# Eight single PSUM banks in place of one group of four and four singles, and experts by blocks of 512 tokens queued beside a line of attentions

## The chip, the core and the metric

The kernel runs on one core of a Trainium2 chip. The core has five engines with queues of their own: PE (TensorE, with its weight loads shown apart as PEld), DVE (VectorE), ACT (ScalarE), POOL (GpSimd) and SP (SyncE, which only issues DMAs here). The metric is device time in microseconds of one execution, lower is better. All arithmetic is in float32, but for a mask that is added in bfloat16.

## The reference

The input is x with 8 sequences of 256 tokens and 128 features, so 2048 rows. Two layers are computed, each an attention and then a mixture of experts. Cut to what matters:

```
# layer 0
q, (k, v) = rope(LN(x) Wqa Wqb), LN(x) Wkva Wkvb       # 16 heads of 8, 4 heads of keys and values
x = x + softmax(q k^T / sqrt(8), causal, per sequence of 256) v Wout + bout
p = softmax(LN(x) gate_W); the two largest of 8 experts, weights scaled to sum 1
o = 0.5 gelu(LN(x) shared_W + shared_b) + sum over the two of weight * (gelu(LN(x) W1[e] + b1[e]) W2[e] + b2[e])
x = x + LN(o) * gamma + beta
# layer 1
xl = LN(x); linear attention over segments of 32 tokens (q, k through elu + 1), normalised, Wo
gates = softmax over the means of earlier segments and a running mean; x += what the gates retrieve
p = softmax(LN(x) gate_w + gate_b); the two largest of 8 experts
x = x + sum over the two of (relu(LN(x) w1[e] + b1[e]) w2[e] + b2[e])
```

The hidden width of an expert is 512. The output has the shape of x.

## The kernel before

Rows are held in four blocks of 512 tokens (`xs[0..3]`, NT = 4 tiles of 128 rows each). A block is two sequences, and layer 0's attention goes sequence by sequence ("row" in the code, eight of them), with heads on the four 32-row groups of the PE.

Attention of layer 0 (`Row`, `attention0`): `maxima` computes the scores of a row once (`scores`, L586, and L592 adds the causal mask), and DVE takes the row maxima from PSUM in one instruction over 2048 columns (L608). `weighted` computes the transposed scores again with the maxima folded in, ACT takes Exp of 2048 columns in one instruction (L637), PE multiplies by the values (L640), DVE copies out (L648), PE picks the columns apart (L651), DVE normalises (L659), PE transposes (L663) and projects (L509). Each row yields three times in `weighted`, and at each of these the maxima of the next row go a step on.

Attention of layer 1 (`attention1`, one block at a time): a projection into four banks (L748), scores per tile into four banks (L877), a mask on DVE over 2048 columns (L881), values (L891, L905), and the retrieval (L938, L946, L952).

Experts: `route0` and `route1` choose two experts for each token. `dispatch` gives each chosen (token, expert) pair a slot of its own in a DRAM buffer (`xg`), where tiles of 128 slots belong to one expert, and POOL scatters the rows there by indirect DMA, 128 rows each (L368). `experts` goes over the tiles: SP reads the number of the tile's expert into a register and loads both weights of that expert, 512 KB in all (L424, L425); PE computes the hidden layer (L431) and the output (L446); ACT (Gelu, and Relu for even chunks) or DVE (Relu for odd chunks) reads the hidden layer out (L441, L439); each four tiles are copied out by DVE (L454) and stored to `yg`. `chosen` gathers them by indirect DMA (L480), and `combine0` or `combine1` adds them to the rows.

Before, the unit of routing is a half of 1024 tokens (HB = 2 blocks). Its number of tiles is fixed: 2048 pairs in 16 tiles plus up to 7 tiles that are begun for an expert and not filled, SL = 23. Two halves in two layers make 92 tiles.

PSUM has eight banks of 512 float32 columns. Before, four of them are one group that scores and layer 1's projection take as a whole, and four are single:

```
ps4 = ctx.enter_context(tc.tile_pool(name="ps4", bufs=1, space=PSUM))
ps1 = ctx.enter_context(tc.tile_pool(name="ps1", bufs=4, space=PSUM))
```

The order of work is set by generators that are woven by hand and by the framework's scheduler, which fixes one order for each engine's queue. `weave(one, other, rate, lead=n)` takes `rate` steps of `other` for each step of `one`, after n steps; a step of `experts` is one tile.

```
weave(first, none, 0.0, stop=HB - 1)
weave(first, chain(moe0(0), second(0)), 1.5, lead=3)
weave(second(1), moe0(1), 2.0, lead=2)
weave(chain(second(2), second(3)), moe1(0), 1.0, lead=2)
weave(moe1(1), finished(0), 0.2, lead=6)
```

So the attention of blocks 0 and 1 runs with no experts beside it, blocks 2 and 3 have experts of the first half beside them, `second(b)` is layer 1 of block b up to its routing, and the experts of the last half stand at the end, with only the last additions behind them.

Of the kernel before, what the change touches and what calls it, by code (L numbers as in the profile page):

```python
# [22 lines left out]

# [16 lines left out]
P = 128  # L40
# [14 lines left out]
HB = 2  # L55
HT = HB * NT
SL = 2 * HT + E - 1
# [9 lines left out]
    "before": P, "ones": P, "cap": E * HT, "upto": E * E, "slot": SL, "index": E,  # L67
# [10 lines left out]
def two_layers(  # L78
# [13 lines left out]
    ps4 = ctx.enter_context(tc.tile_pool(name="ps4", bufs=1, space=PSUM))  # L92
    ps1 = ctx.enter_context(tc.tile_pool(name="ps1", bufs=4, space=PSUM))
# [10 lines left out]
    def quad():  # L104

        return tl(ps4, [P, G, 512], "sc")
# [90 lines left out]
    for h in range(NBLK // HB):  # L197
# [66 lines left out]
    def small(tag, shape=(P, NT, E)):  # L264
        return tl(sm, list(shape), tag)
# [43 lines left out]
    class Half:  # L309


        def __init__(self, h):
            self.h = h
            self.rows = tl(wk, [P, HT, D], "hrows")
            self.hots = tl(wk, [P, 2, HT, E], "hhots")
            self.gates = tl(wk, [P, 2, HT], "hgates")

    def dispatch(half, b1s):

        h1, h2 = half.hots[:, 0], half.hots[:, 1]  # L320
        m, tot = small("chosen", (P, HT, E)), small("total", (P, E))
# [3 lines left out]
        rank = pr[:, 0 : HT * E].rearrange("p (t e) -> p t e", e=E)  # L325
        nc.tensor.matmul(rank, lhsT=const("before"), rhs=m, start=True, stop=False)
        for t in range(HT - 1):
            n = HT - 1 - t
            nc.tensor.matmul(
                rank[:, t + 1 :, :], lhsT=const("ones"),  # L330
                rhs=m[:, t, :].unsqueeze(1).to_broadcast([P, n, E]),
                start=False, stop=(t == HT - 2),
            )
# [3 lines left out]
        c3, tiles = small("cap3", (P, E, HT)), small("tiles", (P, E))  # L337
        nc.vector.tensor_tensor(
            c3, last(pc[:, 0:E], HT), const("cap").rearrange("p (e c) -> p e c", e=E), ALU.is_gt
        )  # L340
        nc.vector.tensor_reduce(tiles, c3, AX.X, ALU.add)
        u3, ends, starts = small("upto3", (P, E, E)), small("ends", (P, E)), small("starts", (P, E))
# [7 lines left out]
        base, pos = small("base", (P, E)), small("pos", (P, HT, E))  # L350
        nc.vector.tensor_scalar_mul(base, starts, float(P))
        nc.vector.tensor_tensor(
            pos, rank, base.unsqueeze(1).to_broadcast([P, HT, E]), ALU.add
        )
        ph, at = small("posk", (P, 2, HT, E)), small("at", (P, 2, HT))
        nc.vector.tensor_tensor(
            ph, half.hots, pos.unsqueeze(1).to_broadcast([P, 2, HT, E]), ALU.mult
        )
        nc.vector.tensor_reduce(at, ph, AX.X, ALU.add)
        half.slots = tl(wk, [P, 2, HT], "slots", mybir.dt.uint32)  # L360
# [5 lines left out]
        for t in range(HT):  # L366
# [22 lines left out]
        half.expert = tl(wk, [P, SL], "expert", mybir.dt.int32)  # L389
        nc.vector.tensor_copy(half.expert, of)  # L390
        half.bias = tl(wk, [P, SL, NC], "bias")
# [83 lines left out]
    def chosen(half, i):  # L475

        yt = tl(wk, [P, 2, NT, D], "yt", bufs=1)
        for t in range(NT):
            for k in range(2):
                nc.gpsimd.indirect_dma_start(  # L480
                    out=yt[:, k, t, :], out_offset=None, in_=yg[half.h][:, :],
                    in_offset=bass.IndirectOffsetOnAxis(
                        ap=half.slots[:, k, i * NT + t : i * NT + t + 1], axis=0
                    ),
                )
# [17 lines left out]
    def project(oT_bank, w):  # L503

        oT = tl(wk, [P, 2 * P], "oT")
        nc.scalar.copy(oT, oT_bank[:, 0 : 2 * P])
# [17 lines left out]
    class Row:  # L524
# [55 lines left out]
        def scores(self, lhsT, rhs, mask):  # L580

            sc = quad()
            for j in range(KVH):
                rows = slice(32 * j, 32 * j + 32)
                with follow(j):
                    nc.tensor.matmul(  # L586
                        sc[:, j, :], lhsT=lhsT[rows], rhs=rhs[rows], start=True, stop=mask is None
                    )
            for j in range(KVH):
                if mask is not None:  # L590
                    with follow(1):
                        nc.tensor.matmul(  # L592
                            sc[:, j, :].rearrange("p (i k) -> p i k", i=G), lhsT=identb, rhs=mask,
# [4 lines left out]
        def maxima(self):  # L598

            for qt in range(2):  # L600
                nms = []
                for kt in range(qt + 1):
                    nm = small(f"nmax{kt}", (P, KVH, G))
# [4 lines left out]
                    nc.vector.tensor_reduce(  # L608
                        nm, sc.rearrange("p j (i k) -> p j i k", i=G), AX.X, ALU.max, negate=True
                    )  # L610
                    nms.append(nm)
                    if kt == qt:
                        dst = self.qx[:, qt, :, :, HD].rearrange("p i j -> p j i")
                        if qt:
                            nc.vector.tensor_tensor(dst, *nms, ALU.min)
                        else:
                            nc.vector.tensor_copy(dst, nms[0])
                    yield

        def weighted(self):  # L620
            oT_bank = bank()
            for qt in range(2):
# [9 lines left out]
                for kt in range(qt + 1):  # L632
# [4 lines left out]
                    nc.scalar.activation(pT, sc, AF.Exp)  # L637
# [12 lines left out]
                for i in range(G):  # L650
# [12 lines left out]
                nc.tensor.transpose(  # L663
                    oT_bank[:, qt * P : (qt + 1) * P], on.rearrange("p j i d -> p (j i d)"), ident
                )
                if qt:
                    pw = project(oT_bank, wout_s)
# [22 lines left out]
    def route0(x, half, i):  # L690
        xn = half.rows[:, i * NT : (i + 1) * NT, :]
# [3 lines left out]
        hots = half.hots[:, :, i * NT : (i + 1) * NT, :]  # L695
# [5 lines left out]
        for k, m in enumerate((m1, m2)):  # L701
            g = half.gates[:, k, i * NT : (i + 1) * NT]
# [17 lines left out]
    def combine0(x, half, i, acc):  # L720
        yt = chosen(half, i)
        for t in range(NT):
            for k in range(2):
                nc.vector.scalar_tensor_tensor(
                    acc[:, t, :], yt[:, k, t, :], half.gates[:, k, i * NT + t : i * NT + t + 1],
# [8 lines left out]
    def attention1(x):  # L734
# [12 lines left out]
        for t in range(NT):  # L747
            nc.tensor.matmul(  # L748
                pp[:, t, :], lhsT=xlT[:, t * P : (t + 1) * P], rhs=wqkvu, start=True, stop=True
            )  # L750
        for t in range(NT):
            nc.scalar.activation(
                s2[:, t].rearrange("p a d -> p (a d)"), pp[:, t, 0 : 2 * D],
# [366 lines left out]
```

## Time and profile before

| what | value |
|---|---|
| time, median of 3 runs | 1099.59 us (1095.2 to 1102.19) |
| the profiled execution, own time | 1101.3 us |
| its span, first to last instruction | 1099.5 us |
| PE busy | 655.6 us (60%), weight loads 444.6 us (40%) |
| DVE busy | 423.0 us (38%) |
| ACT busy | 243.8 us (22%) |
| POOL busy | 211.5 us (19%) |
| mean granted PE clock | 0.697 of full speed |
| DMA | 76.35 MB, mean 69 GB/s |

The page lists, for each line of the kernel, how often an instruction ran, its busy time and mean duration, and the idle time just before it with what ended it. A 40-slice strip shows when each engine was busy and which clock the PE was granted. Windows give the same numbers for stretches that the reader chooses, in microseconds from the span's start; waits list who waited for whom. A busy share over the whole span mixes stages with different limits, so the stages are read one by one.

### The profile page before, as it was taken

How to read it: one execution, taken by the hardware profiler on the slowest of the kernel's cores; microseconds unless marked ns; L12 is line 12 of the kernel's file. 1: busy time of each engine (PE TensorE's matmuls, PEld its weight loads, DVE VectorE, ACT ScalarE, POOL GpSimd, SP SyncE). 2: the span in 40 equal slices, each digit the busy share in tenths (PEclk: the TensorE clock that was granted, in tenths of full speed). 3: DMA queues.
4: the chain of work that ended last, by engine and by line, in shares of the span. 5: the costliest groups of instructions: out<-in, count | busy, mean ns of one | idle time of the engine just before them, and what ended most of it. 6: DMA issues, size and time to landing. Idle time of an engine off the chain costs nothing.

```text
span 1099.5 us, 11701 instructions
## 1 busy us (share of the span) xinstructions
PE 655.6 (60%) x4154; PEld 444.6 (40%) x4170; DVE 423.0 (38%) x1121; ACT 243.8 (22%) x505; POOL 211.5 (19%) x267
## 2 busy tenths in 40 slices
PE   3666555655566677775138649873059759730970
PEld 2222221324122454465115427773037647630970
DVE  4422433235131513041246545442247657541431
ACT  1212121201213434431121014341022122200320
POOL 5000100003300000006440220104721120166005
PEclk9856557655565868876665559995559869955995
DMA  7000000001200222314400004743204413214861
GB/s 213 1 0 1 0 1 1 1 1 52 82 0 20 77 58 58 89 53 129 133 14 1 1 0 129 206 117 112 62 6 135 125 46 87 66 48 134 261 207 55
DMA packets 103786, 76.35 MB, mean 69 GB/s; under 512 B 7520, under 2 KB 89776, under 8 KB 103728
## 3 DMA queue, kind: packets, MB, share of 16 engines
q1 hardware_dynamic: 98304, 66.04, 20.8%
q0 software_dynamic: 4096, 8.40, 2.4%
q10 hardware_dynamic: 1328, 1.17, 0.4%
q8 instruction: 33, 0.54, 0.2%
q14 instruction: 25, 0.20, 0.1%
HBM read 61.30 MB, written 14.29 MB: 69 GB/s over the span
## 4 chain that ended last, share of the span: by engine, by line
PE 48%; DVE 18%; POOL 10%; ACT 9%; issue 8%; DMA 5%; another core or an unknown queue 1%; SPq 0%; POOLq 0%; ACTq 0%; DVEq 0%
PE sc L586 7%; PE mm L431 7%; PE mm L446 6%; DVE nmax L608 5%; POOL yt L480 4%; ACT at L637 4%; PE sc L592 3%; PE mm L640 3%; POOL xg L368 3%; PE sc L748 2%; PE sc L877 2%; PE mm L891 2%; DMA w<-in_w 2%; PE mm L497 2%; PE mm L905 1%
## 5 line engine op out<-in xcount | busy, mean ns | idle before, releaser
L441 ACT ACTIVATE hT<-mm,bias 128x128 f32<-128x128 f32 x276 | 84.9, 371 | 234.9 <-PE mm L431 198.1
L446 PE MATMUL mm<-w,hT 128*128 128x128 f32 x736 | 114.1, 295 | 18.4 <-issue 11.8
L431 PE MATMUL mm<-xrT,w 128*128 128x128 f32 x736 | 117.1, 314 | 6.9 <-DVE xrT L415 6.0
L431 PEld LDWEIGHTS mm<-xrT,w 128*128 128x128 f32 x736 | 106.3, 224 | 17.9 <-DVE xrT L415 10.4
L446 PEld LDWEIGHTS mm<-w,hT 128*128 128x128 f32 x736 | 100.8, 206 | 26.0 <-issue 13.7
L608 DVE TENSOR_REDUCE nmax<-sc 128x16 f32<-128x2048 f32 x24 | 55.0, 2291 | 109.4 <-PE sc L586 71.7
L480 POOL DMA_INDIRECT yt<-yg,slots x64 | 62.3, 974 | 102.9 <-DMA yg<-ys 58.9
L368 POOL DMA_INDIRECT xg<-hrows,slots x64 | 66.6, 1040 | 79.1 <-DVE slots L361 60.8
L640 PE MATMUL mm<-at,vx 128*32 128x512 f32 x192 | 37.7, 871 | 48.9 <-ACT at L637 48.9
L637 ACT ACTIVATE at<-sc 128x2048 f32<-128x2048 f32 x24 | 45.1, 1877 | 81.7 <-PE sc L592 69.7
L586 PE MATMUL sc<-qm,kxT 32*128 32x512 f32 x192 | 42.6, 970 | 25.5 <-DVE nmax L608 16.6
L223 POOL TENSOR_SCALAR rsqrt<-mv 128x4 f32<-128x4 f32 (+1 forms) x24 | 6.1, 254 | 256.2 <-DVE mv L233 251.1
L648 DVE COPY os<-mm 128x512 f32<-128x512 f32 x16 | 11.1, 691 | 113.4 <-PE mm L640 102.0
L251 PE MATMUL mm<-ident,xl 128*128 128x128 f32 x16 | 4.1, 404 | 80.9 <-DVE xl L240 80.9
L955 POOL TENSOR_TENSOR x<-x,hr 128x128 f32<-128x128 f32 x16 | 7.4, 465 | 229.8 <-DVE x L928 216.2
L439 DVE TENSOR_SCALAR hT<-mm,bias 128x128 f32<-128x128 f32 x92 | 31.4, 348 | 36.5 <-ACT hT L441 36.2
L586 PE MATMUL sc<-km,qT 32*128 32x512 f32 x192 | 43.0, 982 | 1.7 <-DVE nmax L608 1.7
L881 DVE TENSOR_TENSOR at<-sc,consts 128x2048 f32<-128x2048 f32 x16 | 36.6, 2287 | 13.7 <-PE sc L877 13.6
L415 DVE COPY xrT<-mm 128x512 f32<-128x512 f32 (+1 forms) x24 | 15.9, 664 | 55.1 <-PE mm L413 34.1
L492 PE MATMUL mm<-ident,gates 128*8 128x128 f32 x32 | 8.1, 407 | 48.5 <-DVE gates L967 21.3
L413 PE MATMUL mm<-ident,xr 128*128 128x128 f32 x92 | 17.8, 325 | 30.8 <-DMA xr<-xg 30.8
L251 PEld LDWEIGHTS mm<-ident,xl 128*128 128x128 f32 x16 | 2.6, 180 | 82.0 <-issue 47.5
(214 smaller groups left out, 1081.3 us busy)
## 6 DMA issues: line engine op xcount, KB each, us to landing
w<-in_w SPq DMA_DIRECT2D x184, 256.0 KB
xr<-xg SPq DMA_DIRECT2D x20, 256.0 KB
yg<-ys SPq DMA_DIRECT2D x20, 256.0 KB
xg<-zero SPq DMA_DIRECT2D x10, 256.0 KB
x<-in_x SPq DMA_DIRECT2D x4, 256.0 KB
xg<-hrows,slots POOLq DMA_INDIRECT x64
yt<-yg,slots POOLq DMA_INDIRECT x64
out<-x SPq DMA_DIRECT2D x4, 256.0 KB
```

Of the source, the lines that this page charges most:

```text
L368: i = nc.gpsimd.indirect_dma_start(out=xg_h[:, :], out_offset=bass.IndirectOffsetOnAxis(ap=half.slots[:, k, t : t + 1], axis=0), in_=half. ...
L431: nc.tensor.matmul(ph[:, c * P : (c + 1) * P], lhsT=w1s[:, c * P : (c + 1) * P], rhs=xrT[:, t * P : (t + 1) * P], start=True, stop=True,)
L439: nc.vector.tensor_scalar(hT[:, c, :], src, bias, 0.0, ALU.add, ALU.max)
L441: nc.scalar.activation(hT[:, c, :], src, func, bias=bias)
L446: nc.tensor.matmul(po[:, t * D : (t + 1) * D], lhsT=hT[:, c, :], rhs=w2s[:, c, :], start=(c == 0), stop=(c == NC - 1),)
L480: nc.gpsimd.indirect_dma_start(out=yt[:, k, t, :], out_offset=None, in_=yg[half.h][:, :], in_offset=bass.IndirectOffsetOnAxis(ap=half.slot ...
L586: nc.tensor.matmul(sc[:, j, :], lhsT=lhsT[rows], rhs=rhs[rows], start=True, stop=mask is None)
L592: nc.tensor.matmul(sc[:, j, :].rearrange("p (i k) -> p i k", i=G), lhsT=identb, rhs=mask, start=False, stop=True,)
L608: nc.vector.tensor_reduce(nm, sc.rearrange("p j (i k) -> p j i k", i=G), AX.X, ALU.max, negate=True)
L637: nc.scalar.activation(pT, sc, AF.Exp)
L640: nc.tensor.matmul(po[32 * j : 32 * j + 32, :], lhsT=self.vx[:, kt, j, :], rhs=pT[:, j, :], start=(kt == 0), stop=(kt == qt),)
L881: nc.vector.tensor_tensor(at.rearrange("p j i k -> p (j i) k"), sc.rearrange("p j (i k) -> p (j i) k", i=G), const("tri").unsqueeze(1).to_ ...
```

## The change

It has two parts.

First, PSUM: the group of four goes, `ps1` has eight buffers, and `quad()` returns four single banks. All that read 2048 columns at once now reads 512 at a time: row maxima (four reductions in place of one), Exp (four in place of one), the mask of layer 1 (four in place of one), the product of the retrieval (four in place of two); the copy of `u` in layer 1 goes from one DVE instruction to four on ACT. The transposes of the normalised heads, which held a bank through a whole row, move into `project`, at the end of the row.

Second, the experts: the unit of routing is a block of 512 tokens, SL = 2 * 4 + 7 = 15 tiles, and four blocks in two layers make 120 tiles. Each block scatters 8 times and gathers 8 times. The experts of a block go into a queue (`Line`), and each step of an attention lets the queue go on by 2.7 tiles (layer 0) or 1.2 tiles (layer 1). A block's experts may start 4 units after it was dispatched; its gather is issued 2 units after its last tile.

```diff
-HB = 2
-HT = HB * NT
-SL = 2 * HT + E - 1
+SL = 2 * NT + E - 1
...
-    ps4 = ctx.enter_context(tc.tile_pool(name="ps4", bufs=1, space=PSUM))
-    ps1 = ctx.enter_context(tc.tile_pool(name="ps1", bufs=4, space=PSUM))
+    ps1 = ctx.enter_context(tc.tile_pool(name="ps1", bufs=8, space=PSUM))
...
     def quad():
-        return tl(ps4, [P, G, 512], "sc")
+        return [bank() for _ in range(G)]
...
-    def project(oT_bank, w):
+    def project(heads, w):
+        pt = bank()
+        for t in range(2):
+            nc.tensor.transpose(pt[:, t * P : (t + 1) * P], heads[t], ident)
...
-                    nc.vector.tensor_reduce(
-                        nm, sc.rearrange("p j (i k) -> p j i k", i=G), AX.X, ALU.max, negate=True
-                    )
+                    for j in range(KVH):
+                        nc.vector.tensor_reduce(
+                            nms[kt][:, j, :], sc[j].rearrange("p (i k) -> p i k", i=G), AX.X,
+                            ALU.max, negate=True,
+                        )
...
-                    nc.scalar.activation(pT, sc, AF.Exp)
+                    for j in range(KVH):
+                        nc.scalar.activation(pT[:, j, :], sc[j], AF.Exp)
...
-        nc.vector.tensor_copy(u, pp[:, :, 3 * D :])
+            nc.scalar.copy(u[:, t, :], pp[t][:, 3 * D :])
...
-                nc.vector.tensor_tensor(
-                    at.rearrange("p j i k -> p (j i) k"),
-                    sc.rearrange("p j (i k) -> p (j i) k", i=G),
-                    const("tri").unsqueeze(1).to_broadcast([P, H, P]), ALU.mult,
-                )
+                for j in range(G):
+                    nc.vector.tensor_tensor(
+                        at[:, j], sc[j].rearrange("p (i k) -> p i k", i=G),
+                        const("tri").unsqueeze(1).to_broadcast([P, G, P]), ALU.mult,
+                    )
...
+    class Line:
+        def __init__(self):
+            self.now, self.credit, self.queue, self.later = 0.0, 0.0, deque(), deque()
+
+        def add(self, steps, then):
+            self.queue.append((self.now + LAG, steps, then))
+
+        def go(self, n):
+            self.now += n
+            while self.later and self.later[0][0] <= self.now:
+                self.later.popleft()[1]()
+            self.credit += n
+            while self.queue and self.queue[0][0] <= self.now and self.credit >= 1.0:
+                _, steps, then = self.queue[0]
+                if next(steps, self) is self:
+                    self.queue.popleft()
+                    self.later.append((self.now + LAG / 2, then))
+                else:
+                    self.credit -= 1.0
+            if not (self.queue and self.queue[0][0] <= self.now):
+                self.credit = 0.0
...
+    def beside(steps, n, stop=None):
+        for mark in steps:
+            line.go(n)
+            if stop is not None and mark == stop:
+                return
+
     first = layer0()
-    weave(first, none, 0.0, stop=HB - 1)
-    weave(first, chain(moe0(0), second(0)), 1.5, lead=3)
-    weave(second(1), moe0(1), 2.0, lead=2)
-    weave(chain(second(2), second(3)), moe1(0), 1.0, lead=2)
-    weave(moe1(1), finished(0), 0.2, lead=6)
-    for _ in finished(1):
-        pass
+    for b in range(NBLK - 1):
+        beside(first, 2.7, b)
+    beside(layer1(0), 1.2)
+    beside(first, 2.7)
+    for b in range(1, NBLK):
+        beside(layer1(b), 1.2)
+    while line.queue or line.later:
+        line.go(1)
```

`layer0` and `layer1` route and dispatch each block and put its experts on the line; the gather of layer 0 is issued when a block's experts are done (`fetch`), and at the end of layer 1 a block is gathered, added and stored (`finish`). The buffers that must live from dispatch to gather (`slots`, `hgates`, `expert`, `bias`) have four copies.

## The prediction

> **What bounds the kernel now.** I read the page's first and second part, then cut the span into its stages with windows, then asked the waits of the stages one by one. First the strip and the windows (columns: stretch, length, then busy time and count of PE, PE's weight loads, DVE, ACT, POOL; granted clock, DMA share, GB/s):
>
> ```profile
> PE 655.6 (60%) x4154; PEld 444.6 (40%) x4170; DVE 423.0 (38%) x1121; ACT 243.8 (22%) x505; POOL 211.5 (19%) x267
> ...
> PE   3666555655566677775138649873059759730970
> ...
> PEclk9856557655565868876665559995559869955995
> ...
> 29.70:148.60 118.90, 72.52 (x304) 30.82 (x307) 41.73 (x98) 22.74 (x32) 5.65 (x12) 0.62 0.00 1
> 148.60:260.00 111.40, 66.46 (x284) 29.69 (x288) 35.88 (x93) 22.09 (x28) 5.65 (x12) 0.62 0.00 0
> ...
> 388.50:500.00 111.50, 83.88 (x469) 61.50 (x474) 31.68 (x86) 45.00 (x77) 4.97 (x5) 0.76 0.24 70
> 500.00:560.00 60.00, 14.89 (x105) 14.27 (x104) 12.18 (x39) 7.56 (x28) 33.74 (x36) 0.61 0.39 115
> 560.00:640.00 80.00, 49.22 (x332) 31.45 (x332) 43.44 (x122) 11.50 (x23) 13.56 (x19) 0.56 0.00 1
> 640.00:745.00 105.00, 84.27 (x731) 69.45 (x731) 48.06 (x116) 38.31 (x114) 8.19 (x12) 0.87 0.41 118
> 745.00:796.00 51.00, 8.23 (x36) 7.42 (x35) 14.20 (x44) 2.43 (x5) 32.78 (x34) 0.50 0.32 93
> 796.00:890.00 94.00, 65.81 (x536) 49.08 (x537) 59.39 (x176) 19.74 (x46) 18.65 (x25) 0.75 0.27 78
> 890.00:985.00 95.00, 68.07 (x563) 54.40 (x561) 50.84 (x123) 18.95 (x47) 21.96 (x26) 0.81 0.25 70
> 985.00:1099.50 114.50, 49.36 (x391) 46.73 (x391) 32.42 (x82) 16.59 (x46) 33.24 (x33) 0.71 0.53 159
> ```
>
> No engine bounds the whole. Three things are to be seen. (a) Where attention runs alone, at 30 to 260 us, PE works 60% of the time at a clock of 0.62; with experts beside it the clock is 0.75 to 0.87. (b) In 500:560 and 745:796 PE does 15 and 8 us of work in 111 us: a half is dispatched or gathered on POOL, and nothing else is ready. (c) The last 114 us hold 16 scatters, 23 tiles of experts and 16 gathers, one after the other.
>
> Then PE's waits in 148.6:260 (one block of layer 0 alone; total us, times, longest), and the experts' rows in 388.5:500 (13 tiles) and 1010:1070 (23 tiles):
>
> ```profile
> PE mm L640 <- ACT at L637: 13.4, 6, 3.3
> PE mm L663 <- DVE on L659: 8.0, 4, 2.1
> ...
> PE sc L586 <- DVE nmax L608: 4.8, 2, 2.4
> ...
> L431 PE MATMUL mm<-xrT,w 128*128 128x128 f32 x107 | 21.7, 375 | 1.6 <-DVE xrT L415 1.6
> L446 PE MATMUL mm<-w,hT 128*128 128x128 f32 x96 | 16.8, 331 | 1.0 <-ACT hT L441 0.9
> ...
> L431 PE MATMUL mm<-xrT,w 128*128 128x128 f32 x184 | 26.8, 291 | 1.5 <-DVE xrT L415 0.8 <-DMA w<-in_w 0.3
> L446 PE MATMUL mm<-w,hT 128*128 128x128 f32 x184 | 26.5, 279 | 0.2 <-DMA w<-in_w 0.2
> ```
>
> PE waits for the whole Exp, for the heads that stand behind a row maximum on DVE, and for the maxima to free the one group of banks. A tile is 8 records of each of two lines: (21.7 + 16.8) / 203 x 16 = 3.0 us of PE beside attention, 53.3 / 23 = 2.3 us in the tail.
>
> **What the Trainium skill says.** "Perfetto Trace Analysis", Optimizing Tensor Performance (Matmuls), tells to rotate matmul groups through different banks so that one's evacuation lies beside the next one's matmuls: the waits above are that fault. The same page, Optimizing Scalar/DVE Operations, puts a fixed cost on each instruction (about 125 ns for DVE and 51 ns for ACT on PSUM) and profiled latency at about twice that: the trace agrees roughly, 2291 ns for 2048 columns (L608) against 690 ns for 512 (L415), so about 155 ns are fixed. "TensorE: Matmul & The Clock Gate", Part 1, has PE at half clock after idle windows and at full clock after busy ones: windows show 0.50 where PE is idle and 0.99 to 1.00 in the dense experts at 1020:1060. "ScalarE: Activation LUTs", What ACT_TABLE_LOAD costs, gives 1283 ns plus a drain for each change of function set: the trace has 1283 ns loads; the drain isn't shown as such.
>
> **The change part by part.** *The split reads.* Row maxima: 24 x 4 instructions; each 690 ns alone, some 610 where the next one follows at once (DVE rows in the timeline overlap by 80 ns), so a set costs 2.5 to 2.8 us in place of 2.29: +0.2 to +0.5 us x 24 = 5 to 12 us of DVE. The mask of layer 1: the same on 16 sets, 4 to 8 us. The retrieval: 32 more instructions of 155 ns or less, 5 us. Exp: 512 columns at some 490 to 600 ns (L630 copies 512 in 589), so 2.0 to 2.4 us a set for 1.88, 3 to 12 us of ACT. All this lies on engines that are 38% and 22% busy; it costs nothing where PE is the bound, and 0.5 us a set where PE waits for the last bank. Function sets: 16 more table loads in the program's order (45 for 29), 20 us of ACT; most come right after Gelu while PE computes scores, as before, and I take them at nothing, up to 1.3 us x 16 = 20 us on the path.
>
> *What the banks free.* Per block of layer 0 (six Exp sets): the maxima no longer stop the scores (4.8 us); the two transposes per row go to the row's end, so PE waits once (of 8.0 us I take 5.5); PE starts on the values after the first 0.6 us of Exp, but then goes at the pace of four Exps, so of 2.2 us a set I take 1.0, 6 us. Sum 16 us in a block alone: 118.9 - 16 = 103 for block 0 (it includes its route).
>
> *A block of layer 0 with 15 tiles.* The model is 388.5:500 with 13 tiles, 111.5 us. Two tiles more at 3.0: 117.5. The same three waits there are 10.0, 5.3 and 1.3 us, of which I take 10: 107.5. PE is then busy 90 of it, and its clock should rise from 0.76 to about 0.83 since the tiles are spread evenly: 90 x (1 - 0.76/0.83) = 7.6. That gives 100. Bounds: 88 (clock 0.9 and all waits gone) to 117.5 (nothing gained).
>
> *A block of layer 1 with 15 tiles.* Three models: 796:890 has 11.5 tiles, +3.5 x 2.7 = 103; 890:985 has 12, +8 = 103; 640:745 has 22, -7 x 2.2 = 89.5. (2.7 and 2.2 are the tile's PE time in those stages.) Mean 98.5, and I take 98. The banks give little here: PE's waits for L881 and L946 were 1 to 4 us a block; the long ones (8.5 us for L492, 5.8 for L773, 5.0 for L251) are the routing chain and the input of the attention, which don't change. Bounds 88 to 106.
>
> *28 more tiles* are in these numbers: 28 x 2.3 to 3.0 = 64 to 84 us of PE, and 14.7 MB more weights. DMA runs at 70 to 118 GB/s beside attention and reached 272 to 301 in the tail, so I cost the loads at nothing beside attention.
>
> *The gaps.* 500:560 and 745:796 go: a block's scatter (8 x 1.27 us, 0.97 and 0.30 between) and its gather have other blocks' work beside them. In the changed program's order each block's dispatch is followed by attention of another block on PE, and the last tiles of a block stand ahead of the next one's route. On POOL the gather of a block stands ahead of the scatter of the next and of the copies that later rows need (L557): 8 x 1.25 = 10 us, beside the 15 us in which the next block is routed. The 18 us stall at 272 to 290 (PE waits for the first half's tiles and POOL) goes likewise; some 5 us may stay per dispatch, which I leave to the range.
>
> *SP.* 160 more queue entries; each tile waits on its register load and four weight buffers, as before.
>
> *The tail.* 114.5 us less 8 scatters (10), 8 tiles at 51/23 = 2.2 us (17.7), 8 gathers (10): 77. Bounds 68 to 95.
>
> **Sum.** Start 29.7 + block 0 103 + three mixed blocks 300 + four of layer 1 392 + tail 77 = 902 us of span. The span before is 1099.5 in an execution of 1101.3, and the median is 1099.6, so 902 stands for the median as it is.
>
> **The rivals.** *Dense PE* (mechanism as forecast, larger): with 15 tiles beside every attention the clock stays near 1 and the chains hide. Block 0 at 90, mixed 88, layer 1 88, tail 72: 29.7 + 90 + 264 + 352 + 72 = 808. For it: 640:745 carried 22 tiles in 105 us at 0.87. Against: the routing waits, 20 us a block, where no tiles are placed. *Stiff order*: queues are fixed, eight banks are shared by experts and scores, so the freed waits return as others (a table load before Exp, a bank held through four tiles). Block 0 119, mixed 117.5, layer 1 104, tail 85: 1002. For it: PE still has the values right behind the scores in the program's order. *Slower*: weights. Each tile's weights are loaded anew and SP issues in order; if a tile beside attention makes PE, and so the attention queued behind, wait w for its weights, 105 tiles cost 902 + 105 w. It decides from w = 2.0 us (1112); at w = 2.5 it gives 1165. For it: the chain has weight transfers of 4.9 and 4.4 us at 1039 and 1056. Against: there DMA was 93 to 98% busy; beside attention 15 tiles x 0.52 MB / 98 us is 80 GB/s, and 640:745 lost only 1.0 us to weights at 22 tiles. *That the change doesn't do what it says*: the order shows tiles between the scores from block 1 on, and no 2048-column reads; I give it no chance of its own.
>
> **How the numbers follow.** Forecast (850 to 960) 0.58; dense (below 850) 0.16; stiff (960 to 1088) 0.19; no change 0.02; slower 0.05. A measurement of this kernel can tell about 1% from no change. Range 820 to 1010: it takes in most of the dense and the stiff case. Faster 0.93, same 0.02, slower 0.05.
>
> **What would show it.** After: PE busy about 650 us at a mean clock above 0.8; no stretch over 15 us without PE before the tail; L608 at 600 to 690 ns x96; the wait L640 <- L637 per set down by about 1 us; blocks of layer 0 about 100 us and of layer 1 about 98; a tail of 77. The forecast is wrong if PE waits for weights in the middle, if a dispatch leaves PE idle over 10 us each time, or if the clock stays below 0.75.

## The result and the profile after

The changed kernel takes 1169.66 us (median of 4, 1156.74 to 1178.15) against 1099.45 us for the kernel before: ratio 1.0603, interval 1.0509 to 1.0697. It is slower by 6%, where 902 us had been forecast. The profiled execution, with a span of 1176.4 us, is the slowest of the four at 1178.15 us and is left out of the ratio, which rests on the other three (1156.74 to 1170.04 us).

First the page of the kernel after: busy times, PE's strip and clock, and groups of PE that changed. The last two lines are the scores of the kernel before.

```profile
PE 879.4 (75%) x4654; PEld 551.2 (47%) x4654; DVE 456.4 (39%) x1385; ACT 301.9 (26%) x693; POOL 212.5 (18%) x267
...
PE   3998868989859988558869896677657866687492
...
PEclk9765655768756869669965887669866986887686
...
L585 PE MATMUL mm<-km,qT 32*128 32x512 f32 x192 | 101.9, 938 | 0.0
L585 PE MATMUL mm<-qm,kxT 32*128 32x512 f32 x192 | 87.2, 848 | 8.9 <-ACT qm L626 8.9
...
L637 PE MATMUL mm<-at,vx 128*32 128x512 f32 x192 | 61.3, 865 | 5.1 <-ACT at L634 5.1
```

```profile
L586 PE MATMUL sc<-km,qT 32*128 32x512 f32 x192 | 43.0, 982 | 1.7 <-DVE nmax L608 1.7
L586 PE MATMUL sc<-qm,kxT 32*128 32x512 f32 x192 | 42.6, 970 | 25.5 <-DVE nmax L608 16.6 <-ACT qm L630 7.1 <-ACT km L520 1.7
```

PE is busy 224 us longer than before (655.6). The experts' two rows account for 90, with 28 tiles more: L427 and L442 are busy 164.9 + 155.9 us, and L431 and L446 were busy 117.1 + 114.1. The scores account for more, 103. L585 does what L586 did, the same 2 x 192 records with a mean that hasn't grown (938 and 848 ns; 982 and 970 before), yet is busy 189 us where L586 was busy 43.0 + 42.6 = 86. Busy time counts a moment once, however many records run in it. With an equal count and a mean that hasn't grown, a doubled busy time says that **records which ran beside each other now run one after the other**.

The timeline of PE shows it. Columns: start, length, line, operation, records; a float32 matmul is two records. One masked set of scores of a row alone, after:

```profile
119.01 2.08 PE L585 MATMUL mm<-km,qT 32*128 32x512 f32 x4
121.02 0.61 PE L591 MATMUL mm<-causb,identb 128*128 128x512 bf16 x1
121.56 2.07 PE L585 MATMUL mm<-km,qT 32*128 32x512 f32 x2
123.56 0.61 PE L591 MATMUL mm<-causb,identb 128*128 128x512 bf16 x1
124.10 2.07 PE L585 MATMUL mm<-km,qT 32*128 32x512 f32 x2
126.10 1.03 PE L591 MATMUL mm<-causb,identb 128*128 128x512 bf16 x2
```

And one before:

```profile
178.00 2.09 PE L586 MATMUL sc<-qm,kxT 32*128 32x512 f32 x8 [2.39 <-DVE nmax L608]
180.42 1.49 PE L592 MATMUL sc<-causTb,identb 128*128 128x512 bf16 x3 [0.33 <-issue]
```

Before, four scores (x8), each on its own 32 rows of the array, take 2.09 us together; with the masks the set takes 3.9 us (one of its masks has no record in this trace). After, the mask of a bank stands between the scores. Two scores still go together, the other two take 2.07 us each, which is as long as the four had taken, and the set takes 8.1 us. These are sets at a low clock; over all 32 masked sets of each trace, the mean from first start to last end is 3.2 us before and 6.9 us after. The order of PE's instructions is the cause: `585 585 591 585 591 585 591 591` in the changed kernel, `586 x4 592 x4` in the kernel before. The source still has a loop over scores and then a loop over masks. But a mask now waits only for the score of its own bank, not for the last access to the one tile of four banks, and it stands under `follow(1)`, which is high priority; so the scheduler can put it earlier. The kernel before has the same `follow(1)` with one tile of four banks, and its order was kept; the first experiment has single banks without it.

The stages, cut at the same instruction of each block (the count of tokens in `dispatch`, L331). Columns as in the windows of the prediction:

```profile
29.70:169.90 140.20, 120.45 (x326) 45.90 (x325) 46.62 (x123) 23.51 (x47) 5.68 (x12) 0.62 0.01 3
169.90:334.80 164.90, 137.61 (x554) 73.98 (x555) 49.24 (x143) 56.29 (x119) 21.82 (x28) 0.69 0.23 67
334.80:503.30 168.50, 136.81 (x555) 75.57 (x555) 52.24 (x166) 56.40 (x119) 24.91 (x30) 0.69 0.22 65
503.30:610.60 107.30, 75.18 (x594) 56.44 (x595) 47.44 (x133) 34.02 (x88) 15.70 (x18) 0.83 0.33 96
610.60:740.00 129.40, 108.21 (x479) 60.87 (x479) 47.38 (x163) 31.77 (x66) 23.52 (x26) 0.72 0.29 85
```

The first three are blocks 0 to 2 of layer 0, then comes layer 1 of block 0, then block 3 of layer 0. The long gaps of PE before the tail are gone, as forecast (34 and 47 us before, at most 13 after), but block 0 alone, without a tile beside it, takes 140 us where 103 were forecast and some 119 were needed before.

### The profile page after: what moved, and what is told of

Read it like the earlier page. It is cut to its first block, busy times and chain, and to the rows that moved or that the text cites. A ratio compares the mean times of both kernels' runs of the same rounds, so it can differ in the third digit from the quotient of the medians.

```text
span 1176.4 us, 13467 instructions
## 1 busy us (share of the span) xinstructions
PE 879.4 (75%) x4654; PEld 551.2 (47%) x4654; DVE 456.4 (39%) x1385; ACT 301.9 (26%) x693; POOL 212.5 (18%) x267
## 4 chain that ended last, share of the span: by engine, by line
PE 61%; DVE 15%; issue 8%; POOL 7%; ACT 4%; DMA 3%; POOLq 0%; SPq 0%; ACTq 0%; DVEq 0%
PE mm L585 15%; PE mm L427 10%; PE mm L442 8%; PE mm L637 5%; PE mm L591 5%; DVE at L876 3%; POOL yt L476 2%; POOL xg L364 2%; PE mm L648 2%; PE mm L885 2%; PE mm L871 1%; PE mm L899 1%; PE mm L493 1%; PE mm L508 1%; POOL rsqrt L220 1%
## 5 line engine op out<-in xcount | busy, mean ns | idle before, releaser
L427 PE MATMUL mm<-xrT,w 128*128 128x128 f32 x960 | 164.9, 327 | 21.9 <-DVE xrT L411 20.9
L442 PE MATMUL mm<-w,hT 128*128 128x128 f32 x960 | 155.9, 302 | 17.1 <-DVE hT L435 6.0
L427 PEld LDWEIGHTS mm<-xrT,w 128*128 128x128 f32 x960 | 147.6, 234 | 38.0 <-DVE xrT L411 26.5
L442 PEld LDWEIGHTS mm<-w,hT 128*128 128x128 f32 x960 | 138.0, 212 | 32.2 <-issue 12.5
L585 PE MATMUL mm<-km,qT 32*128 32x512 f32 x192 | 101.9, 938 | 0.0
L585 PE MATMUL mm<-qm,kxT 32*128 32x512 f32 x192 | 87.2, 848 | 8.9 <-ACT qm L626 8.9
L608 DVE TENSOR_REDUCE nmax<-mm 128x4 f32<-128x512 f32 x64 | 41.1, 685 | 94.8 <-PE mm L585 72.4
L634 ACT ACTIVATE at<-mm 128x512 f32<-128x512 f32 x96 | 53.0, 598 | 66.9 <-PE mm L591 53.5
L645 DVE COPY os<-mm 128x512 f32<-128x512 f32 x16 | 11.1, 692 | 115.6 <-PE mm L637 115.6
L885 PE MATMUL mm<-at,va1z 128*32 128x128 f32 x512 | 37.7, 288 | 18.7 <-DVE at L876 18.6
L876 DVE TENSOR_TENSOR at<-mm,consts 128x512 f32<-128x512 f32 x64 | 40.1, 683 | 17.0 <-PE mm L871 16.9
```

Of the source, the lines that this page charges most:

```text
L427: nc.tensor.matmul(ph[:, c * P : (c + 1) * P], lhsT=w1s[:, c * P : (c + 1) * P], rhs=xrT[:, t * P : (t + 1) * P], start=True, stop=True,)
L442: nc.tensor.matmul(po[:, t * D : (t + 1) * D], lhsT=hT[:, c, :], rhs=w2s[:, c, :], start=(c == 0), stop=(c == NC - 1),)
L585: nc.tensor.matmul(sc[j], lhsT=lhsT[rows], rhs=rhs[rows], start=True, stop=mask is None)
L608: nc.vector.tensor_reduce(nms[kt][:, j, :], sc[j].rearrange("p (i k) -> p i k", i=G), AX.X, ALU.max, negate=True,)
L634: nc.scalar.activation(pT[:, j, :], sc[j], AF.Exp)
L876: nc.vector.tensor_tensor(at[:, j], sc[j].rearrange("p (i k) -> p i k", i=G), const("tri").unsqueeze(1).to_broadcast([P, G, P]), ALU.mult,)
```

## The experiments

Each ratio is to the kernel before as it was timed beside that run (medians of 1094 to 1104 us), so ratios compare better across experiments than times do.

**The masks put back behind the four scores (`masks_after`).** The changed kernel with one edit:

```diff
-                    with follow(1):
-                        nc.tensor.matmul(
+                    nc.tensor.matmul(
                             sc[j]..., lhsT=identb, rhs=mask, start=False, stop=True)
```

> The changed kernel with one edit: the four causal masks of a set of scores (L591) come behind all four scores (L585) on PE, not between them. Theory (row groups): the four scores of a set use four different 32-row groups of PE and run beside each other, 2.0 us for all four; with a full-array mask between them they run one after the other, 2.0 us each, so a masked set takes 8 us for 4 us. 32 masked sets times 3 to 4 us is 100 to 130 us: I expect 1060 us (1030 to 1090), and L585's busy time down from 189 to 85 to 100 us. Rival (28 more tiles of experts, their weights and PE time): the edit takes nothing of that away, so 1150 to 1170. Rival (eight banks shared by scores and experts hold each other up): also 1150 to 1170.

Measured: 1057.13 us, ratio to before 0.956 (0.949 to 0.963). The page's busy times, the groups of the scores, and a set in PE's timeline:

```profile
PE 724.2 (69%) x4654; PEld 504.0 (48%) x4654; DVE 449.9 (43%) x1385; ACT 298.0 (28%) x693; POOL 212.4 (20%) x267
```

```profile
L585 PE MATMUL mm<-qm,kxT 32*128 32x512 f32 x192 | 34.6, 723 | 8.9 <-ACT qm L625 8.9
L585 PE MATMUL mm<-km,qT 32*128 32x512 f32 x192 | 33.7, 757 | 0.0
```

```profile
102.89 2.09 PE L585 MATMUL mm<-km,qT 32*128 32x512 f32 x8
104.91 1.41 PE L590 MATMUL mm<-causb,identb 128*128 128x512 bf16 x4
```

The order of the masks alone is worth 113 us (1169.7 to 1057.1), and turns a loss into a gain of 4.4%. The scores' busy time falls from 189 to 68 us, and the mean masked set from 6.9 to 2.7 us, which over 32 sets is 132 us; the spans differ by 122. Everything else of the change is still there.

**The masks put between the scores in the kernel before (`before_masks_between`).** Only the second loop's head is taken out, so each mask is issued behind its score:

```diff
                         sc[:, j, :], lhsT=lhsT[rows], rhs=rhs[rows], start=True, stop=mask is None
-            for j in range(KVH):
                 if mask is not None:
```

> The kernel before with one edit: each causal mask directly behind its score (one loop for two), so that on PE a full-array mask stands between the scores of the four row groups. One group of four banks, halves and weaving as before. Theory (row groups): each of the 32 masked sets goes from 3.9 to 8 to 10 us, so 1210 us (1180 to 1260), and L586 busy from 86 to 180 to 200 us. Rival (the order of the masks doesn't matter, the loss came with the single banks): 1095 to 1110.

Measured: 1308.82 us, ratio 1.1959 (1.1866 to 1.2052). The timeline, and a window over the attention that runs alone:

```profile
169.26 2.07 PE L586 MATMUL sc<-qm,kxT 32*128 32x512 f32 x2 [2.41 <-DVE nmax L607]
171.80 2.07 PE L586 MATMUL sc<-qm,kxT 32*128 32x512 f32 x2 [0.47 <-issue]
173.80 0.61 PE L591 MATMUL sc<-causTb,identb 128*128 128x512 bf16 x1
174.34 2.07 PE L586 MATMUL sc<-qm,kxT 32*128 32x512 f32 x2
176.34 0.61 PE L591 MATMUL sc<-causTb,identb 128*128 128x512 bf16 x1
176.88 2.07 PE L586 MATMUL sc<-qm,kxT 32*128 32x512 f32 x2
178.88 0.61 PE L591 MATMUL sc<-causTb,identb 128*128 128x512 bf16 x1
```

```profile
30.00:300.00 270.00, 207.84 (x454) 73.51 (x460) 59.24 (x129) 33.93 (x47) 6.70 (x16) 0.53 0.00 0
```

The defect alone, with no other change, costs 215 us. Here no two scores are left adjacent, so each of the four takes 2.07 us; this masked set runs from 169.26 to 179.49, 10.2 us (one mask has no record). There are 32 masked sets (four for each of eight rows); their mean goes from 3.2 to 9.5 us in the traces, and 32 x 6.3 = 202 us, nearly the whole of the loss. The scores are busy 277 us (140.1 + 136.9) where 86 were needed and 180 to 200 had been expected. The whole loss was also more than expected: 1210 us had allowed some 3.5 us a set.

**Each part of the change alone.** `banks_only` has the eight single banks and the experts by halves as before; `blocks_only` has the experts by blocks of 512 with PSUM as before; `banks_masks_after` is `banks_only` with the same edit as `masks_after`.

```diff
# banks_only
-    ps4 = ctx.enter_context(tc.tile_pool(name="ps4", bufs=1, space=PSUM))
-    ps1 = ctx.enter_context(tc.tile_pool(name="ps1", bufs=4, space=PSUM))
+    ps1 = ctx.enter_context(tc.tile_pool(name="ps1", bufs=8, space=PSUM))
...
# blocks_only
-HB = 2
-SL = 2 * HT + E - 1
+SL = 2 * NT + E - 1
...
```

> The kernel before with the first part of the change alone: eight single banks, reads of 512 columns, transposes in project, masks where the change has them (between the scores); halves of 1024 tokens and the old weaving. (Four small buffers have one copy, so that it fits.) Theory (row groups): the loss sits in this part, +100 to 130 us from the scores less 20 to 40 us that the freed banks give: 1160 to 1190 us, and L588 busy some 190 us. Rival (tiles): this part adds no tile, so it is no slower than before, 1050 to 1100.

> The kernel before with the second part alone: experts by blocks of 512 tokens, 120 tiles for 92, queued on the line; PSUM as before with one group of four. Theory (row groups): the scores stay beside each other, so nothing of the loss is here; the gaps of 60 and 51 us go and the tail shortens, against 28 tiles: 1000 us (960 to 1050). Rival (tiles): the 28 tiles and their weights are the loss, 1130 to 1180.

> As banks_only, but with the four masks behind the four scores. Theory (row groups): only what the banks give is left, 1060 us (1040 to 1085), below the kernel before. Rival (the split reads cost more than the banks give): 1100 to 1130, above the kernel before.

| kernel | us | ratio to before | interval |
|---|---|---|---|
| banks_only | 1192.08 | 1.0821 | 1.0783 to 1.0858 |
| banks_masks_after | 1073.96 | 0.9778 | 0.9731 to 0.9825 |
| blocks_only | 1046.78 | 0.9497 | 0.946 to 0.9534 |
| masks_after (both parts) | 1057.13 | 0.956 | 0.949 to 0.963 |

All of the loss is in the banks' part, and in it the order of the masks is 118 us. Two gains, 27.6 us for the mended banks and 54.8 for the blocks, make 44.5 together where their sum is 82: one part takes something back from the other. The stages say where. The four blocks of layer 1 take 464 us in `masks_after` and 414 in `blocks_only`, whose four banks are one tile; from the start to the dispatch of layer 0's third block it is 389 against 430. So the part with the banks, masks mended, helps layer 0 and hurts layer 1.

**Why the banks' part hurts layer 1.** The values of layer 1 (L884 here) start after the mask of their own bank and go at DVE's pace. `layer1_values_last` is `masks_after` with the inner loop over the banks reversed in layer 1, so that the first of the values waits for the last mask; `both_values_last` does the same in layer 0 too, where the values wait for Exp.

```diff
-                    for j in range(G):
-                        with follow(i + j):
+                    for n, j in enumerate(reversed(range(G))):
+                        with follow(i + n):
```

> As masks_after, with one edit in layer 1: of the sixteen products with the values (L884) those come first whose mask product comes last on DVE, so that PE starts them when all four are there and runs the four column groups beside each other, and other work can stand ahead of them. Theory (split reads let PE start too early and stand still between the four parts): L884's busy time from 38 to 20 to 24 us, its wait for DVE from 18.6 to about 6, a block of layer 1 by 6 to 10 us shorter: 1025 us (1010 to 1040). Rival (DVE's four instructions bound that stretch anyway): 1050 to 1060.

> As layer1_values_last, and the same in layer 0: the product with the values that needs the last Exp comes first (L636). Theory (early start): L636's busy time from 62 to 38 to 45 us; since nothing stands ready to fill the wait for the last Exp, no more than 0 to 10 us on the whole below layer1_values_last. Rival (in layer 0 the early start is a gain): 5 to 15 us slower than layer1_values_last.

Measured: 1064.33 us (0.9727, 0.9655 to 0.9798) and 1094.56 us (1.0016, 0.9981 to 1.005). The groups of `masks_after`, of `layer1_values_last`, and the same line in `blocks_only` (L887 there); the number behind `<-DVE` is the wait for the mask:

```profile
L884 PE MATMUL mm<-at,va1z 128*32 128x128 f32 x512 | 37.9, 289 | 18.8 <-DVE at L875 18.6 <-DMA w<-in_w 0.2
```

```profile
L884 PE MATMUL mm<-at,va1z 128*32 128x128 f32 x512 | 19.3, 296 | 28.0 <-DVE at L875 28.0
```

```profile
L887 PE MATMUL mm<-at,va1z 128*32 128x128 f32 x512 | 18.3, 287 | 6.2 <-DVE at L877 6.2
```

Busy and wait are 56.7, 47.3 and 24.5 us. The reversal brings the values side by side again (37.9 to 19.3 us) but PE waits longer, and the time is no better (0.973 for 0.956): the theory that it would gain fell. The timeline of `layer1_values_last` shows where PE stands still: scores, one group of an expert's matmuls, and then the values, which wait until DVE is through four masks.

```profile
662.73 1.14 PE L870 MATMUL mm<-pqm,kT 32*128 32x512 f32 x8
663.80 1.16 PE L442 MATMUL mm<-w,hT 128*128 128x128 f32 x8
666.43 1.08 PE L884 MATMUL mm<-at,va1z 128*32 128x128 f32 x32 [1.47 <-DVE at L875]
```

This suggests that it isn't the first of the values that is early but all of them: their place in PE's order leaves too little work ahead of them. In layer 0 the early start is worth more than was expected: without it the values' busy time falls from 61 to 28 us, but PE's wait for Exp goes from 8 to 38 us, the scores `km,qT` from 33 to 45, and the kernel loses 30 us.

**Fewer tiles (`tiles_12_of_15`).** `masks_after` with the last three of a block's 15 tiles left out, and zeros in their place.

```diff
+SLC = 12
...
-        for s in range(SL + 1):
-            if s < SL:
+        for s in range(SLC + 1):
+            if s < SLC:
```

> As masks_after, but the last 3 of the 15 tiles of each block are left out (their rows come out as zeros): 96 tiles for 120, close to the 92 of the kernel before. Theory (beside attention PE is full, so a tile costs its whole PE time of 2.3 to 2.7 us): 24 tiles fewer give 55 to 65 us, 995 us (985 to 1010). Rival (the tiles fill waits of the attention, as the prediction had it): less than 0.5 us a tile outside the tail's three, 1035 to 1050.

Measured: 1007.19 us (0.9197, 0.9126 to 0.9267), 40 us below `masks_after` by the ratios and 49 by the spans: 24 tiles at 1.7 to 2.0 us. The gain isn't even: blocks 1 and 2 of layer 0 stay at 128 and 136 us, block 3 falls from 119.6 to 102, layer 1 from 464 to 447 in all, the tail from 82 to 68. The total lies inside the theory's range (985 to 1010), but its reason doesn't hold everywhere. In blocks 1 and 2 the three tiles cost nothing: PE has 109 of 1108 records fewer there and is busy as long, 186.2 us for 186.9, at a lower clock: 0.82 and 0.76 where it was 0.86 and 0.84.

**One table of functions (`one_table`).** `masks_after` with Exp in the place of Gelu, in the tiles and in `route0`.

```diff
-        nc.scalar.activation(acc, acc, AF.Gelu)
+        nc.scalar.activation(acc, acc, AF.Exp)
...
-                line.add(experts(half, w1_0, w2_0, AF.Gelu), fetch)
+                line.add(experts(half, w1_0, w2_0, AF.Exp), fetch)
```

> This is masks_after with Exp in the place of Gelu in the experts of layer 0, so ScalarE keeps one table of functions through layer 0; it leaves the expert's activation as another function. masks_after loads a table 45 times at 1.28 us, and five or six of these in each mixed block of layer 0 stood in the chain of waits. Theory (exposed loads are part of why a mixed block took 120 to 135 us where 100 were forecast): three mixed blocks lose 7 to 12 us each, 1025 to 1035 us, ratio to before 0.93 to 0.94. Rival (the loads lie beside TensorE's work, which sets the pace of these blocks): 1050 to 1060 us, ratio 0.955 to 0.965.

Measured: 1038.42 us (0.9408, 0.9358 to 0.9458), between the two theories: some 17 us below `masks_after` as ratios. Blocks 1, 2 and 3 of layer 0 lose 4.3, 4.1 and 3.4 us each, not 7 to 12. All loads but one are gone. These 44 loads of 1.28 us are 56 us of ACT, and 17 us of time went with them, so most were hidden; the prediction had 0 to 20 us for the 16 that the change adds.

**Two banks in a tile (`score_pairs`), and the scores kept together (`score_pairs_together`).** If layer 1 suffers from four short reads, pairs of banks should help it. The first kernel has `masks_after`'s scores in two tiles of two banks, read 1024 columns at a time; the second has two edits more, in layer 0:

```diff
 # score_pairs
-    ps1 = ... bufs=8
+    ps2 = ... bufs=2    # tiles of two banks, for quad()
+    ps1 = ... bufs=4
 # score_pairs_together
-            for j in range(KVH):                     # scores
+            for n, j in enumerate((2, 3, 0, 1)):
...
-                        with follow(j):              # values
+                        with follow(0):
```

> This is masks_after with the four score banks as two tiles of two banks, so one Vector or Scalar instruction reads 1024 columns again: the causal multiply of layer 1 is two instructions instead of four. Theory (in layer 1 four short multiplies at 0.68 us pace the values; two at about 1.2 us each have one access cost less each and release two heads at a time): layer-1 blocks lose 3 to 6 us each, 25 us over five blocks; layer 0's blocks stay within 10 us of masks_after: 1025 to 1045 us. Rival (with fewer tiles to hold, the order in layer 0 puts values between the scores of the next set, and a matmul over all rows between scores takes their concurrency as the masks did): 1080 to 1150 us.

> This is score_pairs with two edits in layer 0 alone: the scores of heads 2 and 3 (the pair of banks that Exp frees last) are computed before those of heads 0 and 1, and the values lose their high priority. PE's order then has four scores of a set side by side, two of the values' matmuls ahead of them and two behind. Theory (the 38 us between what score_pairs should have given and what it gave are the concurrency of the scores, lost to values between them): the scores' busy time falls from 96 us to below 75, the three mixed blocks of layer 0 and the first return to 125, 128, 135 and 120 us, layer 1 keeps its 30 us, 1015 to 1035 us, ratio to before 0.92 to 0.94, below every version so far that computes the reference. Rival (layer 0 was slower in score_pairs because four banks, not eight, hold its scores, so sets wait for Exp and the maxima to free them): 1050 to 1080 us, with the scores' busy time down but new waits of PE for Exp and the maxima.

Measured: 1077.02 us (0.9765, 0.972 to 0.981) and 1023.72 us (0.936, 0.9283 to 0.9437). Scores of `score_pairs` and a piece of its timeline, then scores and layer 1's values of `score_pairs_together`:

```profile
L593 PE MATMUL sc<-km,qT 32*128 32x512 f32 x192 | 61.0, 768 | 1.1 <-DVE qx L615 0.7 <-DVE nmax L615 0.5
L593 PE MATMUL sc<-qm,kxT 32*128 32x512 f32 x192 | 35.3, 776 | 9.1 <-ACT qm L634 9.1
```

```profile
86.69 1.13 PE L593 MATMUL sc<-km,qT 32*128 32x512 f32 x6
87.75 1.04 PE L645 MATMUL mm<-at,vx 128*32 128x512 f32 x2
88.73 1.12 PE L593 MATMUL sc<-km,qT 32*128 32x512 f32 x2
```

```profile
L593 PE MATMUL sc<-km,qT 32*128 32x512 f32 x192 | 41.7, 758 | 8.1 <-ACT at L642 7.0 <-DVE qx L615 0.7 <-DVE nmax L615 0.5
L593 PE MATMUL sc<-qm,kxT 32*128 32x512 f32 x192 | 37.3, 804 | 10.2 <-ACT qm L634 9.1 <-ACT at L642 1.1
...
L894 PE MATMUL mm<-at,va1z 128*32 128x128 f32 x512 | 25.4, 315 | 4.4 <-DVE at L884 4.2
```

Both theories on `score_pairs` were right at once: its layer-1 blocks take 433 us (464 in `masks_after`), and layer 0 lost more than that, since values stood between the scores of the next set: the scores that are computed beside the values (`km,qT`) are busy 61 us, the others 35. In the timeline three scores take 1.13 us together, and the fourth, behind one of the values, 1.12 us by itself. With the pair that Exp frees last computed first, the four scores stand together again, their busy time falls from 96 to 79 us (below 75 was expected), and layer 1 keeps its gain (430 us). The scores are not all of the 50 us between the two versions: the values' own busy time (L645) falls from 80 to 48 us. Some 8 us of new waits for Exp before the scores are what the rival had named. Nor is the size of the reads the only thing that pairs change for layer 1: their four banks are kept for the attentions, and not shared with the experts as the eight are. Which of the two gives the 31 us was not tried. In the timeline of `score_pairs_together` other matmuls stand between layer 1's scores and values, and PE doesn't wait:

```profile
655.74 1.14 PE L879 MATMUL sc<-pqm,kT 32*128 32x512 f32 x8
656.81 1.08 PE L908 MATMUL mm<-consts,rope 128*128 128x36 f32 x8
657.73 1.14 PE L435 MATMUL mm<-xrT,w 128*128 128x128 f32 x8
658.79 1.60 PE L894 MATMUL mm<-at,va1z 128*32 128x128 f32 x32
```

This version is the fastest measured here that does the whole computation, 6.4% below the kernel before.

## Why the prediction was wrong, point by point

The forecast was a sum of stages, and the miss can be told in the same terms. The spans, each from its own profiled execution:

| stage | forecast | after | masks_after |
|---|---|---|---|
| start | 29.7 | 29.7 | 29.7 |
| block 0 of layer 0 | 103 | 140.2 | 95.7 |
| blocks 1, 2, 3 of layer 0 | 300 | 164.9 + 168.5 + 129.4 | 128.0 + 135.3 + 119.6 |
| four blocks of layer 1 | 392 | 107.3 + 122.9 + 118.9 + 114.3 | 107.8 + 122.5 + 119.2 + 114.3 |
| tail | 77 | 80.3 | 82 |
| sum | 902 | 1176 | 1054 |

Of the 274 us that are missing, 122 stand between the last two columns (113 by the medians), all of it in layer 0: that is the order of the masks. The other 152 are sizes: layer 0's mixed blocks (83), layer 1's (72), and -2 for block 0 and the tail together. So the forecast would have been too low with the masks in order as well.

1. **The step that failed: "What the banks free".** It counted what PE no longer waits for, and put the change of the scores' own time at nothing. Instead a masked set of scores went from 3.9 to 8.1 us where the clock was low, the scores' busy time went from 86 to 189 us, and the order that did this cost 113 us of the kernel. What it did count held: 16 us were forecast for a block alone, and with the masks mended it is 19 (111.4 to 92.5 us in `banks_masks_after`, block 1). The dependence that went was also what had held the masks behind the last score. The rival "That the change doesn't do what it says" was dismissed on tiles between the scores and on the reads of 512 columns; the order of scores and masks on PE wasn't weighed. "Stiff order" named the values behind the scores, not the masks between them, and stopped at 1002. The Trainium skill, "TensorE: Matmul & The Clock Gate", Part 3: Packing small matmuls, says that matmuls on different 32-row tiles of the array run concurrently, with 3.07 times the speed measured for four; and that matmuls start and end in the order of the program. The trace agrees, and is nearer to four: four scores in 2.09 us, one in 2.07. That one matmul over all rows between them ends the concurrency, the page doesn't say; the runs show it with masks (`before_masks_between`, and `masks_after` the other way round) and with values (`score_pairs`).
2. **Mis-sized: "A block of layer 0 with 15 tiles", 100 us; measured 120 to 135 with the masks mended.** The model 388.5:500 was a light stretch. The instructions of the row maxima before, in the window of block 1 and in the model's:

```profile
L608 DVE TENSOR_REDUCE nmax<-sc x6: 2290/2292/2292, 165.2 to 236.7; 128x16 f32<-128x2048 f32 x6
```

```profile
L608 DVE TENSOR_REDUCE nmax<-sc x3: 2292/2292/2292, 405.7 to 431.0; 128x16 f32<-128x2048 f32 x3
```

   It holds half of the maxima, and none of the projections of the next rows (L537 runs seven times in the former window, never in the latter). A better base was a block alone. With the mended banks it takes 92.5 us (`banks_masks_after`, block 1):

```profile
125.00:217.50 92.50, 68.35 (x299) 32.13 (x299) 36.87 (x108) 23.21 (x46) 5.60 (x12) 0.78 0.00 0
```

   With 15 tiles at the 2.3 to 3.0 us that the prediction had for a tile, that gives 127 to 137.5, and 128 and 135 were measured. That fits tiles that add their whole time, but leaving three of them out gained nothing in these two blocks; which chain holds them is not settled. Exposed table loads are 4 us of it (`one_table`).
3. **Mis-sized: "A block of layer 1 with 15 tiles", 98 us; measured 108 to 122.** With one tile of four banks it is 95.5 to 109.5, mean 103.5 (`blocks_only`), so the models were short by 5.5 us a block; the banks' part costs 12.4 more, of which the pairs of `score_pairs` give 7.7 back. The prediction had the split mask as 4 to 8 us of DVE over the run, beside other work. DVE's time was right (L875 684 ns x 64 is 7 us above 16 x 2287 ns); the place was wrong, since PE's values stand behind it in order: wait and busy time of that line are 24.5 us in `blocks_only`, 56.7 in `masks_after` and 29.8 in `score_pairs_together`.
4. **Right.** Block 0 with the masks mended (96 for 103), the tail (82 for 77), no stretch over 15 us without PE in the middle (the longest is 13 us after and 14 in `masks_after`), and weights: in `masks_after` the hidden layer's matmuls wait 0.2 us for them in all, so the rival "Slower: weights" has nothing in it. That rival came near the measured time (1165) by a cost that isn't there. Of the signs of being wrong, a clock below 0.75 came in two of the four executions (0.740 and 0.746; 0.757 and 0.763 in the others), and with both parts of the change it passes 0.8 only once the masks are mended (0.817).

## What to carry to other kernels

Before splitting a tile or giving part of its work a higher priority, list the order of each engine's queue before and after, and look at groups that run side by side: in this kernel matmuls on row groups of the array had to stay adjacent, and a dependence that looks like a fault may be what keeps them so. When busy time grows while count and mean stay, concurrency was lost (86 to 189 us here); the timeline shows it in one set. A stage that serves as a model for a forecast must hold the same work: count its instructions by line before scaling it.

The advice of the Trainium skill that the prediction rested on ("Perfetto Trace Analysis", Optimizing Tensor Performance), to rotate matmul groups through banks, holds here only with that order kept: 0.9778 with the masks behind the scores, 1.0821 with the masks between them.

## What the hardware showed that was not expected

A busy PE was not a fast PE. The Trainium skill, "TensorE: Matmul & The Clock Gate", Part 1, has the clock follow how busy PE has been. Block 0 after has PE busy 120.45 of 140.2 us, 86%, at a clock of 0.62; with the scores together it is busy 71.41 of 95.65 us, 75%, at 0.84:

```profile
29.70:125.35 95.65, 71.41 (x324) 32.07 (x321) 45.16 (x123) 22.89 (x48) 5.67 (x12) 0.84 0.01 4
```

In `before_masks_between`, from 30 to 300 us, it is 77% busy at 0.53. So in these runs single matmuls on 32 of 128 rows filled PE's busy time without raising its clock. Whether the clock follows the used part of the array was not tried by itself; these runs only show that the busy share of the profile doesn't predict it. Matmuls that the change of order leaves alone are slower too: the 128 records that pick columns apart (L648, L647 in `masks_after`) have a mean of 336 ns after and 290 ns in `masks_after`. The masks take 64 us after (34.2 + 29.9) and 39 us in `masks_after` (19.3 + 19.3); how much of that is the clock, and how much that most of them stand alone after, is not separated.
